# Moving steps of VectorE and ScalarE work between the turns of a Strassen-tiled graph layer

## The chip, the cores and the metric

The kernel runs on one core of a Trainium2 chip. The metric is the device time of one launch in microseconds. A core has a matrix engine (TensorE, "PE" in the profile, with its weight loads as "PEld"), VectorE ("DVE"), ScalarE ("ACT"), GpSimd ("POOL") and SyncE ("SP", which only issues DMAs here). Each engine has its own queue of instructions, and they meet at semaphores.

## The reference

Two pre-norm layers over 16 batches of a 1024 x 512 node matrix share one 1024 x 1024 adjacency matrix. All is float32.

```
# layer 0
h = relu(layernorm(x))
x = x + (adj @ h) @ W0 + bias
# layer 1: graph attention
h = relu(layernorm(x)) @ W1
e = leaky_relu(s1[:, None] + s2[None, :], 0.2) * adj     # s1, s2 = h @ a1, h @ a2
x = x + elu(softmax(e, axis=2) @ h + beta * h)
```

The change lies in layer 0 and in what is prepared beside it.

## The kernel before, in words

**Products.** Every product of two matrices is one level of Strassen-Winograd: seven products p1 to p7 of half-size blocks. In layer 0, from batch 1 on, the adjacency product adj @ h is two levels deep (`products_a2`): each of its p1 to p7 is again seven products r1 to r7. The weight product (`Weighted`) is one level deep and takes its products in the order p1, p5, p6, p2, p7, p3, p4.

**Steps.** The adjacency product of a batch b is a loop of 28 steps k. A step is two turns of the matrix engine; a turn is one of the r products. p1 and p2 share steps 0 to 6, p6 and p5 steps 7 to 13, p7 and p3 steps 14 to 20. In steps 21 to 27 p4 alternates with the first product of the weights. The other six products of the weights (`rest`) follow in `layer0_b` as steps 2 to 13. Batch 0 has the plain product `products_a` with 14 steps of its own.

**What follows a turn.** r1, r5 and r7 are copied out of PSUM by ScalarE into a small tile `y_pNt`; r6 and r7 are added to it by VectorE; two further adds of VectorE put the inner result into its bank. `ReadA` (line 128) then reads the banks of p1 to p7 out to C11, C12, C21, C22 and forms S1, S2, S4 for the weight product. S3 is `ReadA.s3` (line 174), one add of a 128 x 512 tile for each half. The PSUM tiles `y_pNy` of the inner products come from a pool of two buffers, so p7's takes over p6's.

**Work beside the product.** `after(k)` calls what a plan has at step k. Plans are tables of (step, function, arguments), written by hand. All engines but the DMA queues keep program order (`InOrder`, line 110), so a plan decides where in the queue of each engine an instruction stands. The plans at hand:

- `plan_out` (line 1090), steps of batch b's adjacency product. It finishes u, the layer 1 input of the batch before: `stats` (sums on ScalarE, then a chain on POOL for the inverse deviation), `relu` (ScalarE), `logits` (VectorE: two multiply-reduce instructions of 128 x 512 a call), `store` and `load_res` (DMAs on SP). Beside these stand `inner_left(b, prod)` (line 415), four adds of 128 x 256 on VectorE that form the sums of the left operand of one inner product, and `begin` (line 572), two copies on ScalarE that put the bias into the banks of the weight product.
- `plan_norm_a` (line 1108) and `plan_norm_b` (line 1115): layer norm of the next batch's h, in the adjacency product and in the rest of the weight product: `h_stats`, `h_relu` (ScalarE), `h_sums` (VectorE, four 128 x 512 adds a call), and the left sums of p1 and p2.
- `plan_first` (line 1067): batch 0, with `begin` for its banks Y and X. `at_end` (line 1086) maps the steps of `plan_norm_a` onto the 14 steps of batch 0.
- `FIRST_A` (line 1160): beside the adjacency product of batch 15 runs the first softmax of layer 1, for blocks g of 128 rows: reload `Rg` (DMA), exponential `Eg` (ScalarE, four instructions), transposes `Vg` (VectorE).
- `EARLY_B` (line 1152): the mask group `Mg` on VectorE in the weight products of batches 5 to 12.

**Names in the profile.** `y_p3t <- y_p3y, in_p` is an add of an inner product, `y_S <- xr, v_bc` a logit reduction, `xr <- xr, nb_u, r_u` the ReLU of u, `y_S <- xr` the statistics of u, `h <- h, nb_h, r_h` the ReLU of h, `y_C <- y_Y` a read of the outer bank Y, `po_Y <- w_c, y_C` a weight product, `in_p <- h` a sum of the left operand. All work is recorded at one helper line, 118; so instructions are told apart by tile.

Of the kernel before, what the change touches and what calls it, by code (L numbers as in the profile page):

```python
# [65 lines left out]
def kernel(  # L66
# [12 lines left out]
    B, N, D = x.shape  # L79
# [21 lines left out]
    def bank(name):  # L101
        return psum.tile([P, 512], F32, tag="ps", name=name)
# [21 lines left out]
    def add(o, i0, i1, op=ALU.add):  # L124
        dve.tensor_tensor(o, i0, i1, op=op)
# [89 lines left out]
    def products_a2(name, inner, weighted, after, s4):  # L215


        read = ReadA(name, None, s4)
        read.s3_now = False
        banks = {}  # L220
        by_name = {p[0]: (n, *p[1:]) for n, p in enumerate(PRODUCTS)}

        def inner_steps(prod):

            _, an, bn, kind, first, last = by_name[prod]
            left, sums, right, ext = inner[prod]
            if first:
                banks[kind, 0], banks[kind, 1] = bank(f"{name}_{kind}0"), bank(f"{name}_{kind}1")  # L230
            i0, i1 = banks[kind, 0], banks[kind, 1]
            yx = psum_y.tile([P, 512], F32, tag="psy", name=f"{name}_{prod}y")
            y, x = yx[:, 0:256], (i0 if first else yx)[:, 256:512]
            t = b4.tile([P, 4, 256], F32, tag="b4", name=f"{name}_{prod}t")
            t5 = sums[:, 3].rearrange("p c d -> p (c d)")
            lefts = {
                "r1": left[:, 0:2, P : 2 * P], "r2": left[:, 2:4, P : 2 * P],
                "r7": left[:, 0:2, 0:P], "r4": left[:, 2:4, 0:P], "r5": sums[:, 0],
                "r6": sums[:, 1], "r3": sums[:, 2],
            }  # L240
            rights = {
                "r1": right[:, 0:2, 0:256], "r7": right[:, 0:2, 256:512],
                "r2": right[:, 2:4, 0:256], "r3": right[:, 2:4, 256:512],
                "r5": ext[0], "r6": ext[1], "r4": ext[2],
            }
            outs = {
                "r1": (y, True), "r4": (i0[:, 0:256], first), "r5": (x, False),
                "r6": (y, False), "r7": (y, False), "r2": (i1[:, 0:256], first),
                "r3": (i1[:, 256:512], False),
            }  # L250

            def step(r):
                o, start = outs[r]
                for k in range(2):
                    pe.matmul(
                        o, lefts[r][:, k, :], rights[r][:, k, :], start=(start and k == 0),
                        stop=(k == 1), skip_group_check=True,
                    )
                if r == "r1":
                    act.copy(t[:, 0, :], y)  # L260
                elif r == "r5":
                    act.copy(t5, x)
                elif r == "r6":
                    add(t[:, 1, :], y, t5)
                elif r == "r7":
                    act.copy(t[:, 2, :], y)
                    if first:
                        i0v = i0.rearrange("p (a n) -> p a n", a=2)
                        add(i0v, i0v, t[:, 2:3, :].to_broadcast([P, 2, 256]))
                    else:  # L270
                        add(t[:, 3, :], y, t5)
                        add(out(0), i0, t[:, 2:4, :].rearrange("p a n -> p (a n)"))
                elif r == "r3":
                    add(out(1), i1, t[:, 0:2, :].rearrange("p a n -> p (a n)"))

            def out(p):
                return read.block("C21", p) if prod == "p4" else banks[kind, p]

            order = "r1 r4 r5 r6 r2 r7 r3" if first else "r1 r2 r5 r4 r6 r3 r7"
            return [partial(step, r) for r in order.split()]  # L280

        def reads(prod, p):
            read(prod, p, banks[by_name[prod][3], p])

        k = 0
        behind = []
        for one, two in (("p1", "p2"), ("p6", "p5"), ("p7", "p3")):
            ones, twos = inner_steps(one), inner_steps(two)
            halves = (0, 1) if one == "p1" else (1, 0)
            turns = ones[0:2] + [t for m in range(5) for t in (twos[m], ones[m + 2])] + twos[5:]  # L290
            for m in range(7):
                turns[2 * m]()
                turns[2 * m + 1]()
                if m == 0:
                    for prod, p in behind:
                        reads(prod, p)
                elif m in (4, 5):
                    reads(one, halves[m - 4])
                after(k + m)
            behind = [(two, p) for p in ((1, 0) if two == "p3" else (0, 1))]  # L300
            k += 7
        inn = inner_steps("p4")
        steps = iter(weighted.steps(0, read.c["C11"]))
        for m in range(7):
            inn[m]()
            if m == 0:
                for prod, p in behind:
                    reads(prod, p)
            elif m > 4:
                read.last(6 - m)  # L310
            next(steps)()
            if m == 3:
                next(steps)()
                read.s3(0)
                read.s3(1)
            after(k + m)
        return read.left()
# [742 lines left out]
    def merged(*plans):  # L1060
        out = {}
        for plan in plans:
            for k, steps in plan.items():
                out.setdefault(k, []).extend(steps)
        return out

    def plan_first():
        return {
            1: [(h_sums, 0, 0), (transpose_adj, 0, 1), (transpose_adj, 1, 0), (h_sums, 0, 1)]
            + [(transpose_adj, 1, 1), (adj_sum, "T1"), (adj_sum, "T2")],  # L1070
            4: [(adj_sum, "T3"), (adj_sum, "T4")],
            5: [(logit_weights, 0), (logit_weights, 1), (inner_right, "p1", 0)],
            6: [(load_x, 1, 0), (load_x, 1, 1), (w_sums, w0_c), (inner_right, "p1", 1), (inner_right, "p2", 0)],
            7: [(inner_right, "p2", 1), (inner_right, "p6", 0), (inner_right, "p6", 1)],
            8: [(inner_right, "p5", 0), (inner_right, "p5", 1)], 9: [(inner_right, "p3", 0)],
            10: [(inner_right, "p4", 0), (inner_right, "p7", 0)],
            12: [(begin, 0, "Y")], 13: [(begin, 0, "X")],
        }

    def steps(*pairs):  # L1080
# [2 lines left out]
            plan.setdefault(k, []).append(tuple(step))  # L1083
        return plan

    def at_end(plan):

        return merged(*({min(10 + (k - 14) // 6 if k > 0 else k, 13): v} for k, v in plan.items()))

    def plan_out(o, b):  # L1090

        return steps(
            (-1, o.keep, 0, 1), (-1, o.keep, 1, 0), (-1, o.keep, 1, 1), (0, o.stats, 0, 1, 0),
            (1, o.stats, 1, 0, 0), (2, o.relu, 0, 0), (3, o.stats, 1, 0, 1),
            (4, o.stats, 0, 1, 1), (7, o.relu, 1, 0), (8, o.relu, 0, 1), (9, o.stats, 1, 1, 0),
            (10, o.stats, 1, 1, 1), (13, o.relu, 1, 1),
            (3, o.store, 0, 0), (8, o.store, 1, 0), (9, o.store, 0, 1), (15, o.store, 1, 1),
            (0, inner_left, b, "p6"), (1, inner_left, b, "p5"),
            (3, o.logits, 0, 0, 0), (4, o.logits, 0, 0, 1), (8, o.logits, 1, 0, 0),
            (9, o.logits, 1, 0, 1), (10, inner_left, b, "p7"), (12, o.logits, 0, 1, 0),  # L1100
            (13, inner_left, b, "p3"), (14, o.logits, 0, 1, 1), (16, inner_left, b, "p4"),
            (17, o.logits, 1, 1, 0), (18, o.logits, 1, 1, 1), (18, o.store_logits),
            (18, begin, b, "Y"), (24, begin, b, "X"),
            (10, load_res, b, 0, 0), (13, load_res, b, 0, 1), (16, load_res, b, 1, 0),
            (19, load_res, b, 1, 1),
        )

    def plan_norm_a(b):
# [6 lines left out]
    def plan_norm_b(b):  # L1115
        return steps(
            (2, new_junk, b), (2, h_stats, b, 2, 0), (3, h_stats, b, 2, 1), (4, h_stats, b, 3, 0),
            (5, h_stats, b, 3, 1), (6, h_relu, b, 2), (7, h_relu, b, 3), (8, h_sums, b, 0),
            (10, h_sums, b, 1), (12, inner_left, b, "p1"), (13, inner_left, b, "p2"),
        )  # L1120

    def plan_softmax(order, s):
# [35 lines left out]
        13: {9: "N n"},  # L1158
    }
    FIRST_A = {  # L1160
        13: "R0", 15: "B E0", 16: "V0 R1", 18: "E1", 19: "V1 R2", 20: "E2 b", 21: "V2 R3",
        22: "E3", 23: "V3 R4", 24: "S", 25: "E4", 26: "V4 R5",
    }
    FIRST_B = {
        2: "E5 R6", 3: "V5 E6 R7", 4: "V6", 5: "E7", 6: "V7 s D", 7: "T1a", 8: "T1b", 11: "d T2a",
# [119 lines left out]
```

## Time and profile before

| | |
|---|---|
| median of three runs | 2309.73 us (2304.13 to 2313.26) |
| the profiled execution's own time | 2313.59 us |
| its span, first to last instruction | 2311.8 us |
| mean granted TensorE clock | 0.995 |
| start of the adjacency product of batch 1, 5, 6, 15 | 98.6, 374.2, 443.1, 1063.3 us |
| start of layer 1 | 1139.3 us |

The profile is of one execution. "Busy" is the share of the span in which an engine has an instruction; matmuls are pipelined and their ends are modelled, so the start of one to the start of the next tells more than their length. A bracket behind a timeline row gives the idle time of the engine ahead of it and what released it. The stretches that matter, with the busy times of the engines in us:

| stretch | length | PE | DVE | ACT | POOL | clock |
|---|---|---|---|---|---|---|
| 57.9 to 98.6: end of batch 0 | 40.70 | 35.58 | 28.22 | 26.18 | 7.46 | 0.92 |
| 98.6 to 1063.3: batches 1 to 14 | 964.70 | 943.29 | 811.84 | 711.87 | 145.41 | 1.00 |
| 1063.3 to 1139.3: batch 15 | 76.00 | 70.35 | 66.91 | 43.59 | 4.71 | 0.96 |
| 1139.3 to 2313: layer 1 | 1173.70 | 1158.23 | 945.11 | 791.98 | 213.62 | 1.00 |

### The profile page before, as it was taken

To read this page: it belongs to the slowest core of one execution; us is meant where nothing else is said; L and a number is where in the kernel's file an instruction comes from. 1 tells how busy PE (TensorE), PEld (TensorE's weight loads), DVE (VectorE), ACT (ScalarE), POOL (GpSimd) and SP (SyncE) were. 2 spreads that over 40 slices of the span, in tenths; PEclk is the share of its full clock that TensorE was granted. 3 is DMA by queue.
4 is the path that set the end of the run, shared out by engine and by line. 5 is a ranking of instruction groups with operands and counts; after the bars stand their busy time and mean duration, and the time that the engine had idled before them with its cause. 6 is when DMAs were issued, how large, how long until landed. Compare 5 with 4: busy or idle time off the path is not lost.

```text
span 2311.8 us, 29827 instructions
## 1 busy us (share of the span) xinstructions
PE 2262.0 (98%) x8524; PEld 1610.3 (70%) x8524; DVE 1895.5 (82%) x4225; ACT 1592.3 (69%) x4256; POOL 379.1 (16%) x553
## 2 busy tenths in 40 slices
PE   9999999999999999999999999999999999999998
PEld 5788888888888888888665566655665556655565
DVE  7788888888888888888888888887888878878774
ACT  3667777777777777777466677676776766767753
POOL 1111111111111111111011222112221122201220
PEclk9999999999999999999999999999999999999999
DMA  6243444343443343443635544555446544455441
GB/s 214 100 138 119 165 134 143 134 142 111 155 158 131 139 140 111 137 146 116 210 120 174 162 145 152 187 166 150 145 164 191 170 132 125 141 185 165 132 129 37
DMA packets 194293, 336.04 MB, mean 145 GB/s; under 512 B 78800, under 2 KB 86992, under 8 KB 194128
## 3 DMA queue, kind: packets, MB, share of 16 engines
q1 hardware_dynamic: 193808, 333.61, 44.5%
q8 instruction: 67, 1.10, 0.2%
q14 instruction: 98, 0.80, 0.1%
q10 hardware_dynamic: 320, 0.52, 0.1%
HBM read 228.33 MB, written 109.91 MB: 146 GB/s over the span
## 4 chain that ended last, share of the span: by engine, by line
PE 71%; DVE 16%; DMA 5%; issue 2%; SPq 2%; ACT 2%; POOL 0%; DVEq 0%; ACTq 0%; POOLq 0%
PE z_Y L118 13%; PE po_Y L118 8%; PE pq_Y L118 8%; PE z_X L118 6%; PE y_Y L118 5%; PE po_X L118 5%; PE pq_X L118 4%; DVE y_S L118 3%; PE z_W L118 3%; PE y_X L118 3%; DMA mask<-maskd 3%; PE y_W L118 3%; PE po_W L118 2%; DVE y_C L118 2%; PE y_p6y L118 2%; PE pq_W L118 2%
## 5 line engine op out<-in xcount | busy, mean ns | idle before, releaser
L118 POOL TENSOR_TENSOR x<-x,r 128x512 f32<-128x512 f32 x120 | 198.5, 1671 | 930.5 <-DMA s2b<-s2d 350.6
L118 ACT ACTIVATE e<-e,nm 128x256 f32<-128x256 f32 x480 | 237.2, 497 | 144.2 <-DVE nm L118 144.2
L118 DVE CUSTOM_DVE_ANT_0 e<-e,mask 128x256 f32<-128x256 f32 x512 | 215.7, 477 | 109.2 <-DMA mask<-maskd 92.3
L118 PE MATMUL z_Y<-pT,ul_U 128*128 128x512 f32 x512 | 224.9, 592 | 0.0
L118 ACT ACTIVATE e<-s2b,s1b 128x256 f32<-128x256 f32 x512 | 216.4, 501 | 0.0
L118 PE MATMUL po_Y<-w_c,y_C 128*128 128x256 f32 x768 | 191.7, 384 | 5.1 <-ACT po_Y L118 5.1
L118 PEld LDWEIGHTS z_Y<-pT,ul_U 128*128 128x128 f32 x512 | 97.3, 190 | 115.6 <-issue 109.1
L118 PE MATMUL pq_Y<-w_c,z_C 128*128 128x256 f32 x768 | 174.3, 380 | 0.7 <-ACT z L118 0.6
L118 DVE CUSTOM_DVE_ANT_0 y_S<-xr,v_bc 128x512 f32<-128x512 f32 x240 | 165.0, 687 | 6.3
L118 PEld LDWEIGHTS po_Y<-w_c,y_C 128*128 128x128 f32 x768 | 148.4, 193 | 26.8 <-ACT po_Y L118 5.9
L118 PEld LDWEIGHTS pq_Y<-w_c,z_C 128*128 128x128 f32 x768 | 145.4, 190 | 28.7 <-issue 7.7
L118 DVE STREAM_TRANSPOSE pT<-e 128x512 f32<-128x512 f32 x240 | 155.6, 686 | 1.0
L118 ACT ACTIVATE y_S<-xr 128x512 f32<-128x512 f32 x120 | 75.5, 629 | 90.9 <-DVE xr L118 90.4
L118 DVE TENSOR_TENSOR xr<-po_Y,xr 128x512 f32<-128x512 f32 x128 | 87.6, 684 | 40.7 <-PE po_Y L118 40.7
L118 ACT ACTIVATE h<-h,nb_h,r_h 128x512 f32<-128x512 f32 (+1 forms) x132 | 97.5, 792 | 33.0 <-POOL nb_h L118 33.0
L118 PE MATMUL z_Y<-pT_T,ul_U 128*128 128x512 f32 x256 | 113.8, 594 | 4.0 <-DVE pT_T L118 3.9
L118 PE MATMUL po_X<-w_c,y_S 128*128 128x256 f32 x512 | 115.7, 379 | 0.0
L118 PE MATMUL pq_X<-w_c,z_S 128*128 128x256 f32 x512 | 115.6, 379 | 0.0
L118 PE MATMUL z_X<-pT_T,ul_S 128*128 128x512 f32 x256 | 112.5, 592 | 0.0
L118 PE MATMUL z_X<-pT,ul_S 128*128 128x512 f32 x256 | 112.5, 592 | 0.0
L118 PE MATMUL z_Y<-pT_T,ul_S 128*128 128x512 f32 x256 | 112.5, 592 | 0.0
L118 PE MATMUL z_W<-pT,ul_U 128*128 128x512 f32 x256 | 112.5, 592 | 0.0
(231 smaller groups left out, 5129.9 us busy)
## 6 DMA issues: line engine op xcount, KB each, us to landing
mask<-maskd SPq DMA_DIRECT2D x128, 512.0 KB
h<-in_x_dram SPq DMA_DIRECT2D x64, 512.0 KB
xr<-in_x_dram SPq DMA_DIRECT2D x256, 128.0 KB
x1d<-xr SPq DMA_DIRECT2D x64, 512.0 KB
ul_U<-ud_U SPq DMA_DIRECT2D x64, 512.0 KB
x<-x1d SPq DMA_DIRECT2D x64, 512.0 KB
out_dram<-x SPq DMA_DIRECT2D x252, 128.0 KB
ud_U<-xr SPq DMA_DIRECT2D x60, 512.0 KB
```

The costliest lines, as they stand in the source:

```text
L118: return lambda *args, **kwargs: tc.keep_in_program_order(f(*args, **kwargs))
```

## The change

Only the places of steps change; each engine has as many instructions as before.

1. In `products_a2` the two S3 adds move from step 24 to step 27, behind the last add of p4.
2. In batch 0 `begin` for bank Y moves from step 12 to 9 and for bank X from 13 to 12, and the norm of the next batch's h is spread over steps 10, 10, 11, 11, 12, 13, 13.
3. In `plan_out` the left sums of p6 and p5 leave steps 0 and 1, and go to steps 12 and 13 of the weight product of the batch before (`plan_norm_b`), where the ReLU, the sums and the left sums of p1 and p2 move up.
4. In `plan_out` the later statistics, the ReLUs, the logits, the stores and the loads of the residual move up by one to four steps; the statistics of u(1,0) begin one step later.
5. In `FIRST_A` the reloads, exponentials and transposes of blocks 1 and 2 move up by a step; block 3's exponential moves back by one.

```diff
             if m == 3:
                 next(steps)()
+            elif m == 6:
                 read.s3(0)
                 read.s3(1)
...
-            8: [(inner_right, "p5", 0), (inner_right, "p5", 1)], 9: [(inner_right, "p3", 0)],
+            8: [(inner_right, "p5", 0), (inner_right, "p5", 1)], 9: [(begin, 0, "Y"), (inner_right, "p3", 0)],
             10: [(inner_right, "p4", 0), (inner_right, "p7", 0)],
-            12: [(begin, 0, "Y")], 13: [(begin, 0, "X")],
+            12: [(begin, 0, "X")],
...
+    AT_END = {15: 10, 17: 10, 19: 11, 21: 11, 20: 12, 22: 13, 23: 13}
+
     def at_end(plan):
-        return merged(*({min(10 + (k - 14) // 6 if k > 0 else k, 13): v} for k, v in plan.items()))
+        return merged(*({AT_END[k]: v} for k, v in plan.items()))
...
-            (1, o.stats, 1, 0, 0), (2, o.relu, 0, 0), (3, o.stats, 1, 0, 1),
-            (4, o.stats, 0, 1, 1), (7, o.relu, 1, 0), (8, o.relu, 0, 1), (9, o.stats, 1, 1, 0),
-            (10, o.stats, 1, 1, 1), (13, o.relu, 1, 1),
-            (3, o.store, 0, 0), (8, o.store, 1, 0), (9, o.store, 0, 1), (15, o.store, 1, 1),
-            (0, inner_left, b, "p6"), (1, inner_left, b, "p5"),
-            (3, o.logits, 0, 0, 0), (4, o.logits, 0, 0, 1), (8, o.logits, 1, 0, 0),
-            (9, o.logits, 1, 0, 1), (10, inner_left, b, "p7"), (12, o.logits, 0, 1, 0),
-            (13, inner_left, b, "p3"), (14, o.logits, 0, 1, 1), (16, inner_left, b, "p4"),
-            (17, o.logits, 1, 1, 0), (18, o.logits, 1, 1, 1), (18, o.store_logits),
+            (1, o.relu, 0, 0), (2, o.stats, 1, 0, 0), (3, o.stats, 1, 0, 1),
+            (4, o.stats, 0, 1, 1), (6, o.relu, 1, 0), (7, o.relu, 0, 1), (8, o.stats, 1, 1, 0),
+            (9, o.stats, 1, 1, 1), (11, o.relu, 1, 1),
+            (3, o.store, 0, 0), (7, o.store, 1, 0), (8, o.store, 0, 1), (13, o.store, 1, 1),
+            (2, o.logits, 0, 0, 0), (3, o.logits, 0, 0, 1), (7, o.logits, 1, 0, 0),
+            (8, o.logits, 1, 0, 1), (9, o.logits, 0, 1, 0), (10, inner_left, b, "p7"),
+            (11, o.logits, 0, 1, 1), (12, inner_left, b, "p3"), (13, o.logits, 1, 1, 0),
+            (14, o.logits, 1, 1, 1), (15, inner_left, b, "p4"), (16, o.store_logits),
             (18, begin, b, "Y"), (24, begin, b, "X"),
-            (10, load_res, b, 0, 0), (13, load_res, b, 0, 1), (16, load_res, b, 1, 0),
-            (19, load_res, b, 1, 1),
+            (9, load_res, b, 0, 0), (12, load_res, b, 0, 1), (15, load_res, b, 1, 0),
+            (18, load_res, b, 1, 1),
...
-            (5, h_stats, b, 3, 1), (6, h_relu, b, 2), (7, h_relu, b, 3), (8, h_sums, b, 0),
-            (10, h_sums, b, 1), (12, inner_left, b, "p1"), (13, inner_left, b, "p2"),
+            (5, h_relu, b, 2), (6, h_stats, b, 3, 1), (6, h_sums, b, 0), (7, h_relu, b, 3),
+            (8, h_sums, b, 1), (9, inner_left, b, "p1"), (10, inner_left, b, "p2"),
+            (12, inner_left, b, "p6"), (13, inner_left, b, "p5"),
...
-        13: "R0", 15: "B E0", 16: "V0 R1", 18: "E1", 19: "V1 R2", 20: "E2 b", 21: "V2 R3",
-        22: "E3", 23: "V3 R4", 24: "S", 25: "E4", 26: "V4 R5",
+        13: "R0", 15: "B E0", 16: "V0 R1", 17: "E1", 18: "V1 R2", 19: "E2", 20: "V2 b", 21: "R3",
+        23: "E3", 24: "V3 R4 S", 25: "E4", 26: "V4 R5",
```

## The prediction, made before the changed kernel was run

> **What bounds the kernel now.** I read the page first (shares of the engines, chain of waits), then a table of stretches, then what TensorE waited for, and last the timeline around the largest waits.
>
> ```profile
> PE 2262.0 (98%) x8524; PEld 1610.3 (70%) x8524; DVE 1895.5 (82%) x4225; ACT 1592.3 (69%) x4256; POOL 379.1 (16%) x553
> PE 71%; DVE 16%; DMA 5%; issue 2%; SPq 2%; ACT 2%; POOL 0%; DVEq 0%; ACTq 0%; POOLq 0%
> ```
>
> Two stretches (length, then busy time and instructions of PE, PEld, DVE, ACT, POOL; clock; DMA share, GB/s):
>
> ```profile
> 374.20:422.50 48.30, 46.77 (x214) 39.98 (x213) 42.39 (x100) 36.75 (x94) 7.94 (x19) 1.00 0.52 175
> 422.50:443.10 20.60, 20.60 (x97) 18.13 (x96) 16.12 (x32) 14.73 (x39) 2.47 (x7) 1.00 0.13 53
> ```
>
> TensorE bounds it. The two stretches are one steady period (batch 5): its adjacency product, where DVE has 42.39 of 48.30 us busy (88%), and the rest of its weight product, where TensorE never idles and DVE has 20.60 - 16.12 = 4.5 us free. The period is 68.90 us. Pure matmul time: a turn of the inner products starts every 0.863 us (timeline), so 49 turns x 0.863 + 56 weight matmuls x 0.4315 = 66.5. So 2.4 us of a period are lost. What TensorE waited for between 60 and 1150 us names the places (waits, in us: total, times, longest):
>
> ```profile
> PE y_p3y L118 <- DVE y_p3t L118: 17.2, 15, 1.6
> PE y_p4y L118 <- DVE y_p4t L118: 5.8, 14, 0.4
> PE po_Y L118 <- ACT po_Y L118: 5.1, 1, 5.1
> PE y_p4y L118 <- ACT y_p4t L118: 3.9, 1, 3.9
> ```
>
> Per batch that is one wait at the last turn of p3 (r7) and one at the last of p4 (r7); then two single waits, in batch 0 and in batch 15. Starts on the timeline give the whole loss, restart included: p3 r7 1.38, p4 r7 0.68, and about 0.36 in small ones at p7 and before p3 r2 and p6 r2; together 2.42 us. Layer 1 starts at 1139.3 and is untouched. The timelines of DVE, TensorE and ACT:
>
> ```profile
> 408.94 0.68 DVE L118 CUSTOM_DVE_ANT_0 y_S<-xr,v_bc 128x512 f32<-128x512 f32 x1
> 409.66 0.69 DVE L118 CUSTOM_DVE_ANT_0 y_S<-xr,v_bc 128x512 f32<-128x512 f32 x1
> 410.81 0.38 DVE L118 TENSOR_TENSOR y_p3t<-y_p3y,in_p 128x256 f32<-128x256 f32 x1
> 411.24 1.13 PE L118 MATMUL y_p3y<-adjT_B,hS 128*128 128x256 f32 x4 [1.11 <-DVE y_p3t L118]
> ...
> 396.41 0.58 ACT L118 COPY y_C<-y_Y 128x512 f32<-128x512 f32 x1 [0.94 <-DVE y_Y L118]
> 396.94 0.37 ACT L118 COPY y_p6t<-y_p6y 128x256 f32<-128x256 f32 x1
> 399.28 1.53 ACT L118 ACTIVATE xr<-xr,nb_u,r_u 128x512 f32<-128x512 f32 x2
> ...
> 69.48 1.52 ACT L118 ACTIVATE h<-h,nb_h,r_h 128x512 f32<-128x512 f32 x2 [2.23 <-POOL nb_h L118]
> 71.37 1.10 ACT L118 COPY po_Y<-bias_bc 128x512 f32<-128x512 f32 x2
> 72.00 6.03 PE L118 MATMUL po_Y<-w_c,y_C 128*128 128x256 f32 x16 [5.12 <-ACT po_Y L118]
> ```
>
> To be seen: the add that p3 r7 needs (410.81) stands behind the two last logit reductions; ACT's copy of p6 r7 (396.94) comes before the ReLU of the last half of u (399.28); the bias copy of batch 0 (71.37) stands behind normalisation of h that waited for POOL.
>
> **What the Trainium skill says.** "PSUM — Partial Sum Buffer", section "Engine vs sequencer instructions": the queues of ScalarE and VectorE are strict FIFO and matmuls start in program order; the trace agrees (410.81 runs behind 1.4 us of logits that no matmul needs). "TensorE: Matmul & The Clock Gate", Part 1: an idle window of about 3.4 us halves the clock. The trace agrees: after waits of 5.12 and 3.87 us the matmuls run at half speed, which costs 2.6 and 2.9 us more; after 1.11 and 1.60 they do not. "Perfetto Trace Analysis", "Identifying the Most-Contended Engine": matmul busy share says little about roofline; here too 98% busy hides 66.5 against 68.9 us, so I go by start times.
>
> **The change part by part.** Instruction counts are equal; all is order.
>
> *Left sums of p6 and p5 into the weight product* (steps 12, 13), h's ReLU and sums one or two steps sooner. Four adds of a group take 1.47 us back to back, two groups 2.9. DVE has 4.5 us free there; the S3 adds of part 2 (2 x 0.60) take 1.2 more, so 20.2 of 20.6: it fits, with 0.4 to spare. Before, DVE caught up with TensorE at about 448.8 of the next product; I get 447.5. The first residual add of p3 slips from 439.1 to 441.3 and with it the first statistics of u on ACT, 2.2 us, where ACT had 5 us idle: nothing in most batches; where a mask group (4 x 0.35 us) also sits on DVE (products of batches 6 to 13) p6 r2 then waits about 0.3 and p3 r2 0.1: 0.4 us in 8 batches.
>
> *S3 behind p4.* Two adds of 0.60 leave DVE's queue ahead of p4 r7's add. Its 0.68 us wait goes, with 0.85 to spare. They now stand ahead of the first residual adds, which no matmul awaits; S3 is wanted at product p7 of the weights, more than 10 us later. Cover: that distance.
>
> *Logits sooner, last pair at steps 13, 14 (before 17, 18).* The two reductions (2 x 0.7) ahead of p3 r7's add are gone: its 1.38 us go, with 0.65 to spare. The small p7 waits go too.
>
> What is late next: ReLU of u(1,1) moves from step 13 to 11, so ahead of ACT's copy of p6 r7; and logits (0,1,0) from 12 to 9, ahead of DVE's add for C12. That add (395.69 before) had 0.76 us idle ahead of it and gets 1.34 more work: it ends at about 397.0 instead of 396.3. ACT behind it: C12 copy to 397.65, two ReLUs (1.42) to 399.1, p6 r7 copy to 399.4, then DVE's add to 399.9. The first turn of p7 takes over that PSUM buffer at 398.44, so it waits 1.5. This is the wait the change adds; queued behind on TensorE is all the rest. DVE alone would give at least 0.4; if POOL's inverse deviation (2.0 us after the statistics, 397.4 before) is later, more. I take 1.5, ends 0.4 and 2.8. With p3 r2's 0.55 and small ones, a batch loses 2.25 against 2.42; with a mask 2.65. Six batches x -0.17 and eight x +0.23: +0.8 us.
>
> Stores and residual loads go with them, one to two steps sooner on SP's queue (0.44 us an issue); no matmul waits for them in batches 1 to 14. In 15 one matters, below.
>
> *Batch 0.* begin Y from step 12 to 9: ACT is idle until 57.91 (it waits for h), so the copy is done at about 53; its banks have been free since p2. TensorE goes on at 66.72 instead of 72.00: -5.28, and -2.6 for the half clock. begin X at step 12, now with the sums of h behind it, ends by about 69, wanted at 70.2. If it were late, up to 3 us would come back. I take -7.9.
>
> *Batch 15 (softmax of layer 1 beside it).* The reloads R share one buffer, so R0, E0, V0, R1, E1, V1, R2 is a chain, about 7 us a link (DMA 3.6 to 5.0, exp group 2.0, transposes 0.7 to 1.7). SP now has the store of u(1,1) ahead of R0 (step 13), and that waits for the ReLU: R0 goes out at about 1090, E0 runs at 1094.6 to 1096.6, V0 ends 1098.3, R1 lands 1102, E1 ends 1104, V1 ends 1105.7. V1 is now at step 18, ahead of the add that p3 r7 wants at 1100.9: a wait of 4.8, with half clock after. E2 then delays a p4 copy less than before (3.87), V3 p4 r7 by 2.7. The rest of the weight product would start near 1121.5 instead of 1118.56: +2.9; ends -3 (transfers land as early as before) and +8 (a second half-clock stretch).
>
> Sum: -7.9 + 0.8 + 2.9 = -4.2 us. The profiled run took 2313.6 (span 2311.8 and 1.8 around it), 3.9 above the median of 2309.73, within the spread of the runs; I apply the sum to the median: 2305.5, so 2306.
>
> **The rivals.** A is the above: in every batch the wait moves from the end of p3 and p4 to the start of p7.
>
> B, real gain: ACT and DVE are less backed up at step 11 than summed, p7 waits 0.4. Then 0.5 + 0.2 lost per batch instead of 2.42, some -1.8 x 14 = -25; with batch 0 and 15, -30: 2280. For it: the free 4.5 us of the weight stretch really take work off the full one, and every wait in the list has its cause moved. Against it: DVE stands at 88% there and the work between 387 and 397 grew.
>
> C, slower, one mechanism: the ReLU at step 11 blocks ACT until POOL has u(1,1)'s deviation. Its statistics end at 395.5 in before; one step sooner by program, but ACT starts u 2.2 us later, so POOL's result comes at 397.4 to 398.7, and every 1 us past 397.65 is 1 us of TensorE in each of 15 batches. At a p7 wait of 2.8: A's -4.2 + 1.3 x 15 = +15.3: 2325. It decides from statistics ending after about 396.5 (a p7 wait of 2.6). For it: the margin is nearly nil. Against: ACT still has 1.4 us idle after the first statistics to catch up in.
>
> **How the numbers follow.** A 0.6, 2295 to 2318 (batch 15's ends, and 0.5 us a batch for the p7 wait); B 0.2, 2268 to 2293; C 0.2, 2317 to 2340. The range 2282 to 2325 leaves out half of B and half of C. I count 0.5%, 11.5 us, as what a measurement can tell: faster is below 2298.2 (B and a tenth of A: 0.27), slower above 2321.3 (most of C and a little of A: 0.18), the same 0.55.
>
> **What would show it.** Waits of p3y on DVE and p4y on DVE almost gone from the list for batches 1 to 14, and a new line of about 15 x 1.4 for p7y behind p6t; the period still 68.7 to 69.2; rows of po_Y in batch 0 starting at about 66.7 with no clock loss; one long wait of p3y in batch 15. Wrong would be: a period below 68 (B) or above 69.8 (C, with ACT's idle before the ReLU ended by POOL), batch 0 still waiting for po_Y, or batch 15 losing over 8 us.

## The result and the profile after

| | before | after |
|---|---|---|
| median of 12 runs each | 2309.65 us (2304.13 to 2313.26) | 2312.10 us (2308.22 to 2315.71) |
| ratio, 95% interval | | 1.0012 [1.0003, 1.0021] |
| span of the profiled execution | 2311.8 us | 2310.0 us |
| start of batch 1, batches 1 to 14, batch 15 | 98.6; 964.7; 76.0 us | 90.9; 967.9; 81.4 us |
| layer 1 | 1172.5 us | 1169.8 us |

The changed kernel is slower by 2.45 us, which is just more than the twelve runs of each are uncertain and far below 0.5%. The two profiled executions show the opposite, 1.8 us less: that of the kernel before took 3.9 us more than its median, that of the changed kernel about its median. Layer 1 alone differs by 2.7 us between them. It is the same program in all kernels here and took between 1168.9 and 1173.1 us in their profiles, in no order that can be seen. So batches are compared by their own lengths, and whole kernels by the medians.

What TensorE waited for between 55 and 1150 us in the changed kernel (total, times, longest, in us):

```profile
PE y_p7y L118 <- DVE y_p6t L118: 16.7, 15, 1.4
PE y_p3y L118 <- DVE y_p3t L118: 5.2, 1, 5.2
PE y_X L118 <- ACT y_C L118: 4.3, 15, 0.3
PE y_Y L118 <- ACT y_C L118: 3.5, 9, 0.4
PE y_p4y L118 <- DVE y_p4t L118: 2.1, 1, 2.1
PE po_Y L118 <- DVE xr L118: 1.1, 2, 0.8
```

The waits at the end of p3 and p4 are gone in batches 1 to 14, and 15 waits of p7 stand in their place. New are also fifteen short waits of y_X and nine of y_Y on a copy to y_C (turn r2 of p3 and of p6), and the 5.2 us of batch 15. The wait of po_Y in batch 0 is gone. One p7 wait in the timelines of the changed kernel (batch 5): ScalarE, POOL, VectorE, TensorE.

```profile
386.15 0.35 ACT L118 COPY in_p<-y_X 128x256 f32<-128x256 f32 x1
388.89 0.59 ACT L118 COPY y_C<-y_Y 128x512 f32<-128x512 f32 x1 [2.39 <-DVE y_Y L118]
389.38 1.52 ACT L118 ACTIVATE xr<-xr,nb_u,r_u 128x512 f32<-128x512 f32 x2
390.80 0.35 ACT L118 COPY y_p6t<-y_p6y 128x256 f32<-128x256 f32 x1
...
387.42 0.22 POOL L118 TENSOR_TENSOR nb_u<-mv_u,r_u 128x2 f32<-128x2 f32 x1
...
391.19 0.42 DVE L118 TENSOR_TENSOR y_p6t<-y_p6y,in_p 128x256 f32<-128x256 f32 x1 [0.99 <-ACT y_p6t L118]
...
391.66 1.13 PE L118 MATMUL y_p7y<-adjT_B,h 128*128 128x256 f32 x4 [1.09 <-DVE y_p6t L118]
```

Read it from the bottom up. TensorE waited for VectorE's add, that for ScalarE's copy of p6 r7 (390.80), and this stood behind the ReLU of u(1,1), the last quarter of u (389.38), which stood behind a copy to C12 that waited 2.39 us for VectorE. For the last 1.25 us of that wait the ReLU could have run: POOL's factor was there at 387.64.

The table of stretches of the changed kernel (length, busy PE, PEld, DVE, ACT, POOL, clock, DMA) has the weight product with a mask group, 18.99 of 21.20 us busy on VectorE:

```profile
482.80:504.00 21.20, 21.20 (x100) 18.64 (x100) 18.99 (x41) 13.03 (x33) 3.03 (x6) 1.00 0.10 40
1058.80:1140.20 81.40, 71.62 (x310) 59.82 (x310) 63.06 (x136) 44.63 (x138) 4.67 (x13) 0.96 0.47 155
```

The second row is batch 15, with a mean clock of 0.96, as before the change.

### The profile page after: what moved, and what is told of

The parts are those of the page before. It is cut to its first block, busy times and chain, and to the rows that moved or that the text cites. A ratio compares the mean times of both kernels' runs of the same rounds, so it can differ in the third digit from the quotient of the medians.

```text
span 2310.0 us, 29805 instructions
## 1 busy us (share of the span) xinstructions
PE 2262.2 (98%) x8524; PEld 1608.5 (70%) x8524; DVE 1894.6 (82%) x4225; ACT 1585.9 (69%) x4256; POOL 372.1 (16%) x553
## 4 chain that ended last, share of the span: by engine, by line
PE 56%; DVE 21%; ACT 13%; DMA 4%; issue 4%; SPq 1%; POOL 1%; DVEq 0%; ACTq 0%
PE z_Y L118 14%; PE pq_Y L118 8%; PE z_X L118 7%; ACT y_S L118 5%; PE pq_X L118 4%; PE y_Y L118 4%; PE z_W L118 4%; DVE in_p L118 4%; PE po_Y L118 3%; PE y_X L118 2%; DVE y_S L118 2%; DVE hS L118 2%; PE y_p4y L118 2%; DVE xr L118 2%; PE pq_W L118 2%
## 5 line engine op out<-in xcount | busy, mean ns | idle before, releaser
L118 PEld LDWEIGHTS po_X<-w_c,y_S 128*128 128x128 f32 x512 | 97.3, 190 | 13.2
```

The costliest lines, as they stand in the source:

```text
L118: return lambda *args, **kwargs: tc.keep_in_program_order(f(*args, **kwargs))
```

## The experiments

All were timed in five rounds against the kernel before on the same chip. The median of the kernel before was 2309.1 to 2309.7 us each time, so the times below are compared as they stand. Long lines of an edit are shortened to the steps that move. "Batch 15" is the time from its first turn to the first product of layer 1 in the profile; the period is that of a batch between.

**E1, batch 0 undone.** begin Y, begin X and the norm steps of batch 1 at their old places.

```diff
-9: [(begin, 0, "Y"), (inner_right, "p3", 0)]
+9: [(inner_right, "p3", 0)]
-12: [(begin, 0, "X")],
+12: [(begin, 0, "Y")], 13: [(begin, 0, "X")],
-{AT_END[k]: v}
+{min(10 + (k - 14) // 6 if k > 0 else k, 13): v}
```

> The changed kernel with the batch 0 part undone (begin Y at step 12, begin X at 13, the norm steps of batch 1 as before). Theory (the parts of the change add up; batch 0 gives 7.7 us, batches 1 to 14 cost 3.2, batch 15 costs 5.4): the 5.1 us wait of po_Y on its bias copy is back, +7.7 us on the changed kernel, about 2320. Rival (what batch 0 gains is lost again further on, where later transfers or POOL set the pace): within 2 us of the changed kernel, 2310 to 2314.

Measured: 2317.48 us, ratio to before 1.0037 [1.0025, 1.0050]; 5.4 above the changed kernel. The parts are separate. By these medians this one is worth less than the 7.7 us between the two profiles. TensorE's timeline in this run and, second, in that of the kernel before:

```profile
70.58 5.13 PE L118 MATMUL po_Y<-w_c,y_C 128*128 128x256 f32 x16 [3.80 <-ACT po_Y L118]
```

```profile
72.00 6.03 PE L118 MATMUL po_Y<-w_c,y_C 128*128 128x256 f32 x16 [5.12 <-ACT po_Y L118]
```

The same wait is 3.80 us here and was 5.12 there. Batch 1 begins at 96.3 us here, and at 98.6 there: the wait is shorter, and so is the half clock after it (16 matmuls in 5.13 instead of 6.03 us). The end of the wait follows the landing of batch 1's x: ScalarE's first statistics of it start at 56.80 here and at 57.91 in the kernel before. POOL's last three instructions ahead of the ReLU took 1.5 us here and 2.1 there. E11, further down, has the old steps of batch 0 too, and there batch 1 begins at 98.6 again.

**E10, the batch 0 part alone** on the kernel before (the same lines the other way round).

> The kernel before with the batch 0 part of the change alone. Theory (E1 is right that the part is worth about 5.4 us in a usual execution, and the parts add up, so all else in the change costs about 8): 2303 to 2305. Rival (the 7.7 us between the two profiles is the usual gain): 2301 to 2302.

Measured: 2303.19 us, 0.9966 [0.9952, 0.9979]: 6.5 below the kernel before. With E1, the medians put the part at 5.4 to 6.5 us, and so all else in the change at a cost of 8 to 9. The interval of this run is wide, 4.8 to 11.1 us, so the 7.7 us of the two profiles are not excluded.

**E3, one ReLU moved.** ReLU of u(1,1) from step 11 to 10 in the changed kernel.

```diff
-(9, o.stats, 1, 1, 1), (11, o.relu, 1, 1),
+(9, o.stats, 1, 1, 1), (10, o.relu, 1, 1),
```

> The changed kernel with one step moved: ReLU of u(1,1) from step 11 to 10, so ahead of ScalarE's copy of C12 instead of behind it. Theory (ScalarE's queue makes p7 wait: it idles 2.39 us for VectorE's add and then runs the ReLU ahead of the copy of p6 r7): the ReLU runs inside that idle time, as POOL's factor is there at 387.6 against the end of the idle time at 388.9; the p7 wait falls from 1.1 to 0.2 to 0.5 us in each of 15 batches: 6 to 12 us faster than the changed kernel, 2300 to 2306. Rival (VectorE's own queue sets p7): wait and time unchanged, within 2 us.

Measured: 2296.47 us, 0.9940 [0.9927, 0.9954], 15.6 below the changed kernel. ScalarE's timeline of E3, the same batch:

```profile
383.18 1.52 ACT L118 ACTIVATE xr<-xr,nb_u,r_u 128x512 f32<-128x512 f32 x2 [1.17 <-POOL nb_u L118]
384.60 0.56 ACT L118 COPY y_C<-y_Y 128x512 f32<-128x512 f32 x1
385.07 0.37 ACT L118 COPY y_p6t<-y_p6y 128x256 f32<-128x256 f32 x1
386.80 0.59 ACT L118 COPY y_C<-y_Y 128x512 f32<-128x512 f32 x1 [1.36 <-DVE y_Y L118]
```

The ReLU now starts as soon as POOL's factor is there, ahead of the copy to C12, and the p6 copy follows 1.89 us after the ReLU's start with no idle time between. The period of batch 5 fell from 68.74 to 67.67 us, in the list one p7 wait of 0.3 us is left of fifteen, and no wait of p3 or p4 came back in batches 1 to 14. The gain is more than was expected, 1.07 us a period. VectorE's queue alone sets almost nothing at p7.

**E4, p5's sums back.** For batches 6 to 15 the left sums of p5 return to step 1 of the adjacency product.

```diff
-(12, inner_left, b, "p6"), (13, inner_left, b, "p5"),
+(12, inner_left, b, "p6"), *([] if b > 5 else [(13, inner_left, b, "p5")]),
...
+*([(1, inner_left, b, "p5")] if b > 5 else []),
```

> The changed kernel with the left sums of p5 back at step 1 of the adjacency product, for batches 6 to 15 only. Theory (in the weight products that also hold a mask group VectorE has no room for both groups of sums; statistics of u start late and p6 r2 waits 0.4 us for the copy of C11): that wait goes in 9 batches, about 4 us faster than the changed kernel. Rival (the sums only move the backlog; VectorE is as late at step 2 with them at step 1): same wait, within 1.5 us, or slower.

Measured: 2313.74 us, 1.0019 [1.0012, 1.0025]; the line of y_Y on y_C stays at 3.5 us in nine waits. The expected gain did not come, but the run cannot say why by its time. VectorE's timeline ahead of batch 6, of the changed kernel and then of E4, shows that the edit left the order of VectorE's queue as it was:

```profile
430.95 0.41 DVE L118 TENSOR_TENSOR in_p<-h 128x256 f32<-128x256 f32 x1
432.41 0.68 DVE L118 TENSOR_TENSOR xr<-po_X,xr 128x512 f32<-128x512 f32 x1
437.74 0.41 DVE L118 TENSOR_TENSOR in_p<-hS 128x256 f32<-128x256 f32 x1
440.13 0.42 DVE L118 TENSOR_TENSOR y_p1t<-y_p1y,in_p 128x256 f32<-128x256 f32 x1 [0.84 <-PE y_p1y L118]
```

```profile
437.69 0.42 DVE L118 TENSOR_TENSOR in_p<-hS 128x256 f32<-128x256 f32 x1
440.06 0.42 DVE L118 TENSOR_TENSOR y_p1t<-y_p1y,in_p 128x256 f32<-128x256 f32 x1 [0.83 <-ACT xr L118]
```

The sums of p5 (437.74, 437.69) come last before the first add of p1 with either plan, so moving them tests nothing. The rows tell more than the time does: the statistics of u start after the first residual add of p3 (432.41). The sums of p5 stand behind it, as do those of p6 (from 435.68), and VectorE idles 0.84 us after both groups. Of the left sums only those of p1 (from 430.95) stand ahead of it.

**E5, order inside the weight product.** E3 with the sums of p1 and p2 two steps later, behind the residual adds of p3.

```diff
-(9, inner_left, b, "p1"), (10, inner_left, b, "p2"),
+(11, inner_left, b, "p1"), (12, inner_left, b, "p2"),
```

> E3 (ReLU of u(1,1) at step 10) with the left sums of p1 and p2 at steps 11 and 12 of the weight product instead of 9 and 10. Theory (these two groups, moved up by the change, stand on VectorE ahead of the residual adds of p3, so that u's first statistics start late; a mask group makes it 2 us too late and p6 r2 waits for the copy of C11): the wait of y_Y on y_C, 0.4 us and 0.2 of restart in 9 batches, is gone: 4 to 6 us faster than E3, 2291 to 2293. Rival (VectorE is late because of its whole load; the order inside the weight product doesn't matter, as in E4): within 1.5 us of E3.

Measured: 2291.38 us, 0.9918 [0.9905, 0.9932], 5.1 below E3. The nine waits are gone. ScalarE's timeline of the changed kernel ahead of batch 6, which starts at 434.68, and then of E5, where it starts at 430.00:

```profile
433.13 0.63 ACT L118 ACTIVATE y_S<-xr 128x512 f32<-128x512 f32 x1 [5.35 <-DVE xr L118]
```

```profile
427.00 0.63 ACT L118 ACTIVATE y_S<-xr 128x512 f32<-128x512 f32 x1 [3.89 <-DVE xr L118]
```

The first statistics of u start 1.55 us ahead of the batch in the changed kernel and 3.01 in E5; without a mask group 2.24 and 3.70; before the change it was 3.98 in both. The gain of 1.46 us is the length of one group of sums, that of p1. So both the order and the mask group count: at 2.24 ScalarE still catches up, at 1.55 it doesn't.

**E6, p3's sums.** E3 with the left sums of p3 at step 13 again, behind the two adds into bank X.

```diff
-(12, inner_left, b, "p3"), (13, o.logits, 1, 1, 0),
+(13, inner_left, b, "p3"), (13, o.logits, 1, 1, 0),
```

> E3 with the left sums of p3 at step 13 instead of 12. Theory (the 0.3 us wait of y_X on y_C in 15 batches, 0.45 with restart, comes from these four adds, 1.47 us, ahead of the two adds into bank X whose result ScalarE copies to C22): the wait goes: 5 to 7 us faster than E3, 2290 to 2292. Rival (the logits of u(0,1) and u(1,1) keep VectorE full there and p3's own r5 or r7 becomes late instead): within 2 us of E3, or slower, with a wait of y_p3y in the list.

Measured: 2290.72 us, 0.9917 [0.9903, 0.9930], 5.8 below E3. The 15 waits of y_X on y_C are gone, and the period of batch 5 is 67.22.

**E2, FIRST_A as before** in the changed kernel.

```diff
-16: "V0 R1", 17: "E1", 18: "V1 R2", 19: "E2", 20: "V2 b", 21: "R3",
-23: "E3", 24: "V3 R4 S", 25: "E4", 26: "V4 R5",
+16: "V0 R1", 18: "E1", 19: "V1 R2", 20: "E2 b", 21: "V2 R3",
+22: "E3", 23: "V3 R4", 24: "S", 25: "E4", 26: "V4 R5",
```

> The changed kernel with FIRST_A as before (E1, V1, E2, V2 a step later). Theory (the transposes V1 stand one step too early in VectorE's queue, ahead of the add that p3 r7 wants): the 5.2 us wait of y_p3y falls below 2 us, a p4 copy waits behind E2 instead as before (about 4 us), batch 15 ends 2 to 5 us sooner. Rival (the reload chain is late because SP's queue has the store of u(1,1) ahead of R0, whatever FIRST_A's later steps are): batch 15 within 1.5 us of the changed kernel.

Measured: 2310.10 us, 1.0001 [0.9993, 1.0009]; batch 15 took 79.2 us. The wait of p3y is gone as the theory had it, but two waits of p4y came, 3.4 and 3.2 us, so most of the loss stays. Neither side was right: against the 80.2 to 81.4 us of batch 15 in the changed kernel, E1 and E4 the order of FIRST_A is 1 to 2 us of it.

**E7, the last logits of batch 15 late.** E3 with the logits of u(1,1) and store_logits of batch 15 alone at steps 17 and 18.

```diff
-(13, o.logits, 1, 1, 0), (14, o.logits, 1, 1, 1), (16, o.store_logits),
+(17 if b == B - 1 else 13, o.logits, 1, 1, 0),
+(18 if b == B - 1 else 14, o.logits, 1, 1, 1), (18 if b == B - 1 else 16, o.store_logits),
```

> E3 with, for batch 15 alone, the logits of u(1,1) and store_logits at steps 17 and 18 as before the change. Theory (batch 15 is late because the moved logits stand on VectorE ahead of the first transposes V0, and the next reload waits for those): V0 about 1.8 us sooner in the batch, every later link too, batch 15 two to four us shorter than in E3 (80.2). Rival (the chain is set by its own links of about 7 us and by SP's queue ahead of R0): batch 15 within 1 us of E3.

Measured: 2294.06 us, 0.9931 [0.9919, 0.9943], 2.4 below E3; batch 15 took 78.5 us against 80.2, a little less of a gain than was expected. The intervals of E3 and E7 overlap, so this rests on the profile: the transposes V0 start 31.1 us into batch 15 instead of 32.5, and the next reload R1 32.5 instead of 33.9. So the logits that the change puts ahead of the first transposes are a part of batch 15's loss.

**E8, all together**: E3 with E5, E6 and E7.

> E3 with the edits of E5, E6 and E7 together. If each works and they add up: 12 to 16 us faster than E3, 2281 to 2285. If VectorE's load is the common limit, the gains overlap: 2288 to 2293, with a new wait at the end of p3.

Measured: 2281.28 us, 0.9875 [0.9861, 0.9888]. The three gains on E3 sum to 13.3 us, together they gave 15.2: they add up. The period is 67.22 us in 13 of 14 batches, against 66.5 of pure matmul time. In the list of waits between 50 and 1140 us of E8 only batch 15 and one p7 wait are left:

```profile
PE y_p3y L118 <- DVE y_p3t L118: 3.2, 1, 3.2
PE y_p4y L118 <- DVE y_p4t L118: 2.5, 1, 2.5
PE y_p7y L118 <- DVE y_p6t L118: 0.3, 1, 0.3
```

**E9, another order in batch 15.** E8 with exponentials and transposes behind the copies and adds of the inner products, and those of block 4 in the weight product.

```diff
-13: "R0", 15: "B E0", 16: "V0 R1", 17: "E1", 18: "V1 R2", 19: "E2", 20: "V2 b", 21: "R3",
-23: "E3", 24: "V3 R4 S", 25: "E4", 26: "V4 R5",
+13: "R0", 15: "B E0", 16: "V0 R1", 19: "R2", 20: "E1", 22: "V1 E2 R3", 23: "V2 b",
+24: "E3", 25: "V3 R4", 26: "S",
...
-2: "E5 R6", 3: "V5 E6 R7", 4: "V6", 5: "E7", 6: "V7 s D",
+2: "E4 R5 R6", 3: "V4 E5 R7", 4: "V5 E6", 5: "V6 E7", 6: "V7 s D",
```

> E8 with another order of the softmax beside batch 15: each exponential and transpose placed behind the copy or add of the inner product that is due in its step (R2 19, E1 20, V1 E2 R3 22, V2 23, E3 24, V3 R4 25, S 26; blocks 4 to 7 in the weight product). Theory (what batch 15 loses, 78.1 us against 67.2 of the others, is exponentials that wait for a reload at the head of ScalarE's queue and transposes at the head of VectorE's, with the half clock after them): batch 15 falls to 69 to 72, 6 to 9 us faster than E8, 2272 to 2276. Rival (the chain of reloads sets the end, so blocks 4 to 7 come later and the first products of layer 1 wait for them): batch 15 at 76 or more, within 2 us of E8.

Measured: 2280.44 us, 0.9869 [0.9856, 0.9883]; batch 15 took 76.3 us against 78.1. The rival is nearer. The waits in the inner products shrink, and new ones in the weight product take their place (the longest waits between 50 and 1140 us of E9):

```profile
PE po_Y L118 <- DVE xr L118: 5.0, 2, 3.2
PE y_p3y L118 <- DVE y_p3t L118: 1.4, 1, 1.4
PE y_p4y L118 <- ACT in_p L118: 1.2, 1, 1.2
```

The rest of the weight product starts 50.0 us into batch 15 instead of 55.8 in E8, but then takes 26.3 us instead of 22.4: of 5.8 us won, 3.9 are lost again.

**E11, S3 alone.** The kernel before with only the two S3 adds behind p4.

```diff
             if m == 3:
                 next(steps)()
+            elif m == 6:
                 read.s3(0)
                 read.s3(1)
```

> The kernel before with the S3 adds behind p4 alone. Theory of the prediction (two adds of 0.60 us stand ahead of the add p4 r7 wants; 0.68 us a batch with restart, in 14 batches): the wait of y_p4y on y_p4t goes, 8 to 10 us faster than before, 2299 to 2301. Rival (the adds only move the backlog to the residual adds and from there to u's statistics in the next product, so p3 r7 waits longer): within 3 us of before, with a larger wait of y_p3y.

Measured: 2300.67 us, 0.9957 [0.9945, 0.9970]: 9.0 below the kernel before. The line of y_p4y on y_p4t is gone, that of y_p3y on y_p3t is unchanged at 17.2 us, and the period is 68.22 instead of 68.90. If the parts add up, as E1 and E10 suggest, this one and batch 0 are worth about 15 us, and items 3 to 5 of the change together cost about 18: an estimate from E10, E11 and the 2.45 us. E3 shows that most of this hangs on the place of one ReLU.

## Why the prediction was wrong, point by point

The forecast was 4.2 us less, by three terms, and 2.45 more was measured. The steps that failed are two of these terms: +0.8 for batches 1 to 14, where 3.2 was measured, and +2.9 for batch 15, where 5.3 was. Nearly all the waits came where they were put, but these costs were too small, by 2.4 us each, and that alone turns -4.2 into +0.6. Batch 0 gave 0.2 to 2.5 us less than its 7.9, which the runs don't settle.

| term | predicted | measured |
|---|---|---|
| batch 0 | -7.9 | -5.4 (E1) to -6.5 (E10) by medians, -7.7 by the two profiles |
| batches 1 to 14 | +0.8 | +3.2 (967.9 - 964.7) |
| batch 15 | +2.9 | about +5.3 |
| sum | -4.2 | +0.8 to +3.1; the medians say +2.45 |

For batch 15 the changed kernel, E1 and E4 have the same order in every queue: 81.4, 80.8 and 80.2 us, 80.8 on average. The kernel before, E10 and, but for the S3 adds, E11 have the old: 76.0, 74.7 and 75.6, so 75.5.

**Batch 0.** "-5.28, and -2.6 for the half clock" is 5.24 and 2.4 in the two profiles, 98.6 against 90.9. Of the three executions with the old steps two began batch 1 at 98.6, and E1 at 96.3; the new steps gave 90.3 to 92.1. The prediction took a wait that ends on a load as a fixed price. The medians make it smaller, by 1.4 to 2.5 us, but the interval of E10 holds 7.9 too, so it is not shown that this term was wrong.

**The p7 wait.** Predicted 1.5 us, by ScalarE's queue; 1.09 us of idle time were found, and 1.36 to 1.37 were lost a batch, since the matmuls after a wait start late (the restart). The bounds said 0.4 for VectorE alone; E3 shows 0.3 (its loss at p7, restart included, from 1.37 down by the period's 1.07). POOL, the price of rival C, came at 387.64, 1.25 us before the C12 copy, so it decided nothing. Batches without a mask group have 68.74 instead of 68.90: -0.16, predicted -0.17.

**The mask batches.** This term was mis-sized: 0.4 us more a batch than others in eight batches was predicted, 0.56 in nine was measured (69.31 against 68.75). Against the kernel before, that is 0.41 instead of 0.23 in eight batches, 1.4 us in all, and 0.45 instead of -0.17 in the ninth, 0.6 us. The last 0.3 us are batch 7, where p7 waited 1.36 us instead of 1.09; why is open. The first slip of u's statistics was put at 2.2 us everywhere; it is 1.74 without and 2.43 with a mask group. The ninth batch is 14: it has no mask group, but the steps N and n of `EARLY_B` on VectorE, which were overlooked. The cause that was named, the first residual add of p3 slipping behind other work, holds: E5 removes it by moving only the sums of p1 and p2. The sums of p6 and p5, for which the prediction counted 20.2 of 20.6 us, are not to blame: they stand behind that add in VectorE's queue (E4's rows). They also ran only after the stretch had ended, and without them VectorE was busy there for 18.99 of 21.20 us, so that sum did not come about.

**Batch 15.** The other mis-sized term is the step "The rest of the weight product would start near 1121.5 instead of 1118.56: +2.9". The waits were right: a wait of 4.8 predicted and 5.2 found at p3, 2.7 and 2.1 at p4, half clock after the first. The rest of the weight product started 58.8 us into the batch instead of 55.3, so 3.5 later against 2.9; on average over the three executions each it is 4.0. Then the prediction stopped: it added nothing behind that point. The timelines of TensorE and VectorE in the changed kernel show what came:

```profile
1117.58 3.62 PE L118 MATMUL po_X<-w_c,y_S 128*128 128x256 f32 x16
1128.95 3.96 PE L118 MATMUL po_Y<-w_c,y_C 128*128 128x256 f32 x16 [0.84 <-DVE xr L118]
1136.62 3.73 PE L118 MATMUL po_Y<-w_c,y_C 128*128 128x256 f32 x16 [0.26 <-DVE xr L118]
...
1127.01 1.30 DVE L118 STREAM_TRANSPOSE pT<-er 128x512 f32<-128x512 f32 x2 [3.28 <-ACT er L118]
1128.24 0.65 DVE L118 TENSOR_TENSOR xr<-po_Y,xr 128x512 f32<-128x512 f32 x1
```

Two products waited for residual adds that stood behind the late transposes and what follows from these; from the first of these rows to layer 1 it took 22.6 us instead of 20.7. In E1 and E4 this part took 21.6 and 21.9 us, and 20.7 in all three executions of the old order. E9 starts it sooner and loses most of the gain there, with waits of 3.2 and 1.8 us for residual adds.

The times of the chain up to V1 came out within 1.3 us of the prediction's, counted from the start of the batch, but its reason for the start did not hold, so the agreement is in part luck. The store did put R0 later, 25.4 us into the batch instead of 23.6. But E0 follows the copies on ScalarE without any wait for its load:

```profile
1088.68 0.39 ACT L118 COPY in_p<-y_p7y 128x256 f32<-128x256 f32 x1
1089.12 0.51 ACT L118 ACTIVATE er<-er,nm 128x256 f32<-128x256 f32 x1
```

In E3 R0 goes out at 23.8 again, and batch 15 still takes 80.2 us, as in E4 with R0 at 25.4: the later R0 is not what costs. E7 shows the moved logits ahead of V0 as 1.7 us of the loss, E2 FIRST_A as 1 to 2; the rest is not divided up.

**S3 and p3's wait.** Right in size: predicted 0.68 a batch for S3, E11 shows 0.68. The removal of the logits ahead of p3 r7 held too: no wait of p3 is left in 14 batches.

**Rival B** (p7 waits only 0.4) described a kernel one step away. With the ReLU at step 10 it is what happens at p7, 12.8 us below the kernel before. That is less than half of B's 30, since r2 of p3 and of p6 still wait, and batch 15 still loses; E8 lies 27.8 below.

## What to carry to other kernels

A step that is moved sooner in a full queue lands ahead of something: look for the instruction of the same engine that now stands behind it and has a matmul waiting, and try the place before the idle time rather than after it. One step of one ReLU was worth 15.6 us here. When a forecast is a difference of terms of similar size, follow each to where the path is free again, and take a wait that varies between executions from more than one profile.

## What was not expected of the hardware

The bias wait of batch 0 was 5.12 us in one execution, and 3.80 and 3.79 in two others (E1 and E11) with the same steps there; and after the same 3.8 us batch 1 began at 96.3 us in E1 and at 98.6 in E11, where the next 16 matmuls took 6.65 us instead of 5.13. The granted clock was at a half for 3.41 us in E1, from 70.06 on, and for 6.83 in E11 and the kernel before. Every half-clock stretch of these profiles that lies in batches 0 to 15 behind such a wait has one of these two lengths. How long it lasts is not given by the wait: after waits of 4.78 us (E4) and 4.86 (E1) in batch 15 it was 3.41 and 6.83.

Nor does the wait alone say whether the clock halves. The prediction reckoned with an idle time of about 3.4 us. From 40 us on, all waits of TensorE of 3.39 us and more were indeed followed by half clock, but a wait of 2.52 us was in E1, E3, E5, E6, E7 and E8 and was not in E4, and one of 3.23 us was in E8 while 3.22 in E2 was not. So a forecast should price a wait of 2.5 to 3.4 us both with and without the half clock.

Layer 1, the same program in all profiles here, spread over 4.2 us (1168.9 to 1173.1). Against that, the periods of batches 1 to 5 agree within 0.02 us between batches of one run and between the runs of the same steps. Over 14 batches that is 0.3 us, where the times of one kernel's twelve runs spread over 7 to 9: a steady stage shows far smaller differences than the whole time does.
